# A two-layer cross-attention kernel: another order of the work of a group in its second layer

## Chip, cores and metric

One core of a Trainium2 chip runs the kernel. The metric is device time in microseconds (us) of one execution. TensorE (PE) multiplies matrices, VectorE (DVE), ScalarE (ACT) and GpSimd (POOL) work elementwise, and SyncE (SP) issues most DMAs.

## What is computed

Sixteen batch rows `x` of 256 positions and 320 channels pass through two cross-attention layers with 20 heads of 16 channels. The context has 256 tokens of 512 channels. Layer 1 (index 0) treats the first 77 tokens as text and the rest as image tokens; layer 2 (index 1) treats the last 4 as image tokens. The second layer, cut to what matters:

```python
q   = heads(hidden_states @ W_q)
k_t = heads(text_ehs @ W_k);  v_t = heads(text_ehs @ W_v)
probs_t  = softmax(einsum('bhsd,bhtd->bhst', q, k_t) * attn_scale)
text_out = einsum('bhst,bhtd->bhsd', probs_t, v_t)
k_ip = heads(ip_ehs @ W_k_ip);  v_ip = heads(ip_ehs @ W_v_ip)
attn_scores = einsum('bhsd,bhnd->bhsn', q, k_ip) * attn_scale
qsem = l2norm(einsum('bhst,bte->bhse', probs_t, text_ehs))
sem  = einsum('bhse,bne->bhsn', qsem, l2norm(ip_ehs))
probs_ip = softmax(attn_scores + 0.5 * sem) * spatial_mask
out = (text_out + einsum('bhsn,bhnd->bhsd', probs_ip, v_ip)) @ W_out + b_out + residual
```

The norm of `qsem` is found without forming it, from the probabilities and the products of tokens with each other (the Gram matrix of the context).

## The kernel before, in words

Each layer works in 80 *groups*: 16 batch rows by 5 groups of four heads. One *slot* of the main loop at the end of `xattn2` advances each of several groups by one stage; slots 0 to 79 are layer 1 (`slot0`), the next 80 and two more are layer 2 (`slot1`). The order of TensorE's instructions is the order in which the code emits them. The queues of the other four engines are ordered by the framework's scheduler, by the dependences and a planned time line, and then run strictly in that order.

In layer 2, a slot `k` holds, in the order of `slot1`:

- `attend1(k - 2)`: the values of the group two slots back. 16 matmuls onto 32-column tiles (L852) multiply the probabilities `P` by the tokens' values, and 8 more (L854, the *zone*) add the column sums of `W`, the norm's products. `settle1` then transposes and divides on VectorE (L898, L901, L902).
- `both1(k, 0)` and `both1(k, 1)`: the two halves of the 64-row work. Each has transposed scores of group `k` (L800, two PSUM banks, exponentials on ScalarE at L811 into `P`) and scores of group `k + 2` (L805), whose row maximum VectorE takes (L806). The scores have one PSUM buffer of two banks (`scores()`, `bufs=1`). Both kinds use 48 to 50 rows, two at a time in the upper and lower 64 rows of the array.
- `norm1(k - 1, u, n)`: the *block products*, the rounded probabilities (`R`) by blocks of the Gram matrix, four matmuls (n = 0) and three (n = 1) for each of two halves u (L839). VectorE multiplies each result by the remainder `W` (L842). The sum of both goes to GpSimd for u = 0 and to VectorE for u = 1 (L844); the zone matmuls read it.
- `rounded1(k, u)`: ScalarE rounds `P` (L829), GpSimd takes the remainder (L830).
- `stacks(k + 4)`: DMAs that load the queries and keys of a later group; `maxima(k + 2)`: two small matmuls (L817), a copy (L819) and two DMAs issued by ScalarE (L821) that put the maxima into the query stack.
- a number between the parts, such as `yield 0.33`, calls `fill`: all steps of the side tasks that are due by then are emitted. Each task has a list of due times: the next rows' keys (`keys1`), tokens' values and Gram matrix (`tokens1`), queries and image scores (`open1`, with the image keys of `image1`, L510), the image softmax (`image_softmax`), and the output projection (`close1`). Their matmuls are called *fillers* below.

Buffers decide what may overlap. The stacks of queries and keys, `qs` and `ks`, have four tiles each (`NR`), which layer 2 uses as eight half stacks in turn. `P` has four tiles, two for a group, so a group's exponentials overwrite the probabilities of the group two back, and `attend1(k - 2)` must come before `both1(k, 0)`:

```python
P[k, u] = buf("P", [128, 2, 2, S], bufs=SIZES["NP"])
```

Of the kernel before, what the change touches and what calls it, by code (L numbers as in the profile page):

```python
# [16 lines left out]
B = 16  # L17
# [31 lines left out]
def xattn2(  # L49
# [212 lines left out]
    wq, wo = [lambda s, k, m=slice(None): wqt[:, s, k, m]], []  # L262


    qs = [const_tile([128, 4, S], f"qs{i}", FR) for i in range(SIZES["NR"])]
    ks = [const_tile([128, 4, S], f"ks{i}", FR) for i in range(SIZES["NR"])]
    ind0 = buf("raw", [128, 512], bufs=SIZES["RAW"], name="ind0")[:2, :S]
    dma(ind0, ind0_d)
    ind0r = buf("mt", [8, S], FR, name="ind0r")[:2]
# [367 lines left out]

    def stacks1(k):
        b, g = divmod(k - NS, NG)
        n = 2 * SIZES["NR"]  # L640
        i = ((NS - SIZES["NR"]) % SIZES["NR"]) * 2 + (k - NS) % n
        Q, K = QK[k] = [x[i // 2 % SIZES["NR"]][:, 2 * (i % 2) : 2 * (i % 2) + 2] for x in (qs, ks)]
        get("k1", b)
        qd = get("o1", b)[0]
        for u in range(2):
            rows = slice(64 * u, 64 * u + XROW)
            hs = slice(4 * g + u, 4 * g + u + 3, 2)
            if k - NS < n:
                dma(K[64 * u + XROW : 64 * u + KS1], w1["ind"])
            dma(K[rows], stack_rows(kd[1][b][:, :, 0])[:, hs])  # L650
            dma(Q[rows], stack_rows(qd)[:, hs])
# [134 lines left out]
    def both1(k, t):  # L786

        a = k + 2 < 2 * NS and QK[k + 2] 
        c = NS <= k < 2 * NS and QK[k]
        if a:  # L790
            if t == 0:
                maxes[k + 2] = buf("mn", [128, 4, 4], FR, bufs=2)[:, :2]
            sp = scores()
        if c:
            st = [bank("T").rearrange("p (h t) -> p h t", h=2) for u in range(2)]
            lo = (0, DUP)[t]
            for j in range(2):
                for u in range(2):
                    rows = slice(64 * u, 64 * u + KS1)
                    mm(st[u][:, j], c[1][rows, j, lo : lo + 128], c[0][rows, j], start=True, stop=True)  # L800
        if a:
            for j in range(2):
                for u in range(2):
                    rows = slice(64 * u, 64 * u + XROW)
                    mm(sp[:, 2 * u + j], a[0][rows, j, t * 128 : (t + 1) * 128], a[1][rows, j], start=True, stop=True)  # L805
            anchor(nc.vector.tensor_reduce(maxes[k + 2][:, t], sp[:, :, :T1], axis=AX.X, op=ALU.max))  # L806
        if c:
            for u in range(2):
                if t == 0:
                    P[k, u] = buf("P", [128, 2, 2, S], bufs=SIZES["NP"])  # L810
                anchor(nc.scalar.activation(P[k, u][:, t], st[u], AF.Exp, scale=SCALE))  # L811

    def maxima1(k):
# [43 lines left out]
    def slot1(k):  # L857
        last = k - 1 if NS < k <= 2 * NS else None
        mine = k < 2 * NS
        if k == NS:  # L860
            yield lambda: maxima(k + 1)
        elif k == NS + 1:
            yield lambda: attend0(k - 2)
        else:
            yield lambda: attend1(k - 2)
        yield lambda: both1(k, 0)
        if last:
            yield lambda: norm1(last, 0, 0)
        yield 0.33
        if last:  # L870
            yield lambda: norm1(last, 0, 1)
        yield lambda: both1(k, 1)
        if mine:
            yield lambda: rounded1(k, 0)
        yield lambda: stacks(k + LEAD)
        if last:
            yield lambda: norm1(last, 1, 0)
        yield 0.67
        if last:
            yield lambda: norm1(last, 1, 1)  # L880
        if mine:
            yield lambda: rounded1(k, 1)
        yield lambda: maxima(k + 2)
        yield 1.0
# [89 lines left out]
    def open1(b):  # L974
# [2 lines left out]
        xs = split(x, tmask[:, 5:6], nc.gpsimd, "hq")  # L977
        yield
        get("w2")
        qh, qd = yield from queries(1, xs)  # L980

        kb = image1(b)
        yield
        sp = bank()[:, :S]
        prod(sp, lambda s, k: kb[:, s, k], lambda s, k: qh[:, s, k], 3)
# [48 lines left out]
    def shifted(n, *times):  # L1034

        return [RAMP(n + t) for t in times]
# [10 lines left out]
    for c in range(B // 2):  # L1047
# [8 lines left out]
        task(("v0", 2 * c + 1), shifted(n, -4, -3.8, -3.4), lambda b=2 * c + 1: values0_(b), *k)  # L1056
        for b, t in ((2 * c, (-7.4, -6.4, -6, -5.4, -5, -4.4, -3.4)), (2 * c + 1, (-2.4, -1.4, -1, -0.8, -0.4, 0, 1.2))):
            task(("s0", b), FIRST["s0"] if b == 1 else shifted(n, *t), lambda b=b: semantic0(b), ("q0", b), ("m0t", b))
            task(("c0", b), shifted(5 * b, *((5.6, 6, 6.6, 7.2, 7.6, 8.2) if b % 2 == 0 else (5.6, 6, 6.6, 7.2, 8.2, 9.2) if b < B - 1 else (6.33, 6.67, 7, 7.67, 8, 8.67))), lambda b=b: close0(b), ("w4", 0))
    for b in range(B):  # L1060
        n = NS + 5 * b
        task(("k1", b), shifted(n, -7, -6.67, -6.33, -5.67, -5, -4.67), lambda b=b: keys1(b), ("w2",), *([("t1", b - 1)] if b else []), *([("w4", 1)] if b > 2 else []))
        task(("t1", b), shifted(n, -3.67, -3, -2.67, -2.33), lambda b=b: tokens1(b), ("k1", b), ("w3", b % 2))
        task(("o1", b), shifted(n, -7.67, -7, -6.67, -5.33, -4.33, -4), lambda b=b: open1(b), ("w7",), ("c0", b), *([("o1", b - 1)] if b else []))
        task(("i1", b), shifted(n, 6.67, 6.67, 6.67, 6.67, 7.33, 7.33, 7.67, 7.67, 8, 8.33), lambda b=b: image_softmax(b, NG - 1 if b == B - 1 else 0), ("gathered", b), ("taken", B + b - 1), *([("i1a",)] if b == B - 1 else []))
        task(("c1", b), shifted(n + (1.67 if b > B - 3 else 0), 8.67, 9, 9.33, 10, 11.67, 13.33), lambda b=b: close1(b), ("i1", b), ("w4", 1))
    task(("i1a",), [2 * NS + 0.1], lambda: image_softmax(B - 1, 0, NG - 1), ("i1", B - 2))
    spread = lambda t, d, n: [t + d * i for i in range(n)]
    thirds = lambda n, t: [t + i // 3 + (0.2, 0.6, 1.0)[i % 3] for i in range(n)]
# [157 lines left out]
```

## Time and profile before

| what | value |
|---|---|
| median of three runs | 1540.75 us (1538.49 to 1541.03) |
| the profiled execution | 1543.74 us, its span 1542.0 us |
| layer 2 in that execution | first scores of layer 2 at 676 us, first transposed scores at 690 us |
| VectorE, ScalarE, GpSimd, share of the span | 78%, 62%, 75% |

The profile's groups are lists of instructions by source line, engine and tile, with the mean length of one. Starts in the timeline are measured; ends of matmuls are modelled. A row in brackets names what ended the idle time in front of it. Line numbers are those of the kernel before.

### The profile page before, as it was taken

The page shows a single profiled execution, that of the slowest core. Times are in us where ns is not written, and L with a number is a line of the kernel's source. Part 1 is how long each engine was busy: PE and PEld are TensorE (multiplying, and loading weights), DVE is VectorE, ACT ScalarE, POOL GpSimd, SP SyncE. Part 2 cuts the span into 40 slices and gives each one's busy share as a digit, 9 for nine tenths or more (in the row PEclk, how much of TensorE's full clock was granted, in tenths as well). Part 3 has the DMA queues.
Part 4 walks back from the last instruction along what each step waited for, and adds up shares of the span by engine and source line. Part 5 has one row for each costly group of instructions (what it writes and reads, how often), then busy time and mean ns, then how long its engine had stood idle before and what let it go on. Part 6 is the DMA issues. An engine that isn't in the chain of part 4 may idle for free.

```text
span 1542.0 us, 35152 instructions
## 1 busy us (share of the span) xinstructions
PE 1480.8 (96%) x12666; PEld 1200.5 (78%) x12666; DVE 1203.0 (78%) x2472; ACT 950.0 (62%) x2073; POOL 1155.2 (75%) x1161
## 2 busy tenths in 40 slices
PE   7889999999999998799999999999999999999997
PEld 6778888888888887677777777777777777777765
DVE  5567677767677779877888888888888888888796
ACT  5567676767677767655655555655555556556553
POOL 3359797979787868797777777777777777777685
PEclk9899999999999999999999999999999999999999
DMA  6756665656565665554443443334243434432301
GB/s 213 179 161 179 164 174 160 189 145 193 151 183 151 183 172 151 146 164 138 144 126 89 131 126 113 113 117 152 82 133 115 138 98 131 127 117 84 105 28 57
DMA packets 205626, 212.82 MB, mean 138 GB/s; under 512 B 28362, under 2 KB 189356, under 8 KB 205452
## 3 DMA queue, kind: packets, MB, share of 16 engines
q1 hardware_dynamic: 203712, 209.27, 46.9%
q8 instruction: 101, 1.65, 0.5%
q10 hardware_dynamic: 1740, 1.30, 0.3%
q14 instruction: 73, 0.60, 0.1%
HBM read 120.91 MB, written 88.18 MB: 136 GB/s over the span
## 4 chain that ended last, share of the span: by engine, by line
PE 86%; DVE 6%; ACT 3%; DMA 2%; issue 1%; POOL 1%; SPq 0%; ACTq 0%; POOLq 0%; DVEq 0%
PE X L212 23%; PE X L839 18%; PE X L532 11%; PE P L723 7%; PE S L662 5%; PE T L685 4%; PE T L800 4%; PE P L852 4%; PE P L854 3%; PE S L805 2%; PE X L960 1%; PE X L581 1%; DVE wt L844 1%; POOL P L691 1%; PE X L670 1%
## 5 line engine op out<-in xcount | busy, mean ns | idle before, releaser
L691 POOL TENSOR_TENSOR P<-P,rs 128x512 f32<-128x512 f32 x320 | 412.7, 1312 | 154.1 <-ACT P L688 114.8
L830 POOL TENSOR_TENSOR wt<-P,ctb 128x512 f32<-128x512 f32 x320 | 418.1, 1322 | 131.2 <-ACT ctb L829 131.0
L839 PE MATMUL X<-ctb,gm 128*128 128x512 f32 x1120 | 330.0, 412 | 0.0
L811 ACT ACTIVATE P<-T 128x512 f32<-128x512 f32 x320 | 174.1, 598 | 107.5 <-PE T L800 106.6
L688 ACT ACTIVATE P<-T 128x512 f32<-128x512 f32 x320 | 174.8, 593 | 101.2 <-PE T L685 91.2
L829 ACT ACTIVATE ctb<-P 128x512 fp32r<-128x512 f32 x320 | 195.4, 632 | 60.0 <-PE X L839 59.5
L839 PEld LDWEIGHTS X<-ctb,gm 128*128 128x128 f32 x1120 | 189.3, 188 | 45.3 <-issue 0.4
L806 DVE TENSOR_REDUCE mn<-S 128x4 fp32r<-128x1008 f32 x160 | 192.0, 1200 | 0.2 <-PE S L805 0.2
L842 DVE TENSOR_TENSOR wt<-X,wt 128x512 f32<-128x512 f32 x240 | 161.9, 679 | 12.1 <-PE X L839 11.1
L664 DVE TENSOR_REDUCE mn<-S 128x4 fp32r<-128x716 f32 x160 | 142.5, 890 | 0.0
L723 PE MATMUL P<-P,vr 128*32 128x256 f32 x1920 | 123.0, 387 | 7.8 <-DVE tmp L740 4.9
L662 PE MATMUL S<-ks,qs 125*128 125x256 f32 x640 | 115.6, 303 | 1.9 <-DVE mn L664 1.9
L532 PE MATMUL X<-hq,wE 128*128 128x256 f32 x768 | 110.4, 288 | 4.5 <-ACT hq L521 3.9
L662 PEld LDWEIGHTS S<-ks,qs 125*128 125x128 f32 x640 | 87.1, 191 | 34.8 <-issue 31.3
L532 PE MATMUL X<-ho,wF 128*128 128x256 f32 x768 | 108.9, 285 | 0.9 <-ACT mt L672 0.5
L532 PEld LDWEIGHTS X<-hq,wE 128*128 128x128 f32 x768 | 103.0, 194 | 8.2 <-ACT hq L521 4.3
L685 PE MATMUL T<-qs,ks 127*128 127x256 f32 x640 | 104.3, 286 | 1.9 <-DVE kst L148 1.9
L212 PE MATMUL X<-cta,wA 128*128 128x252 f32 (+1 forms) x720 | 100.2, 285 | 5.9 <-ACT wA L147 5.5
L532 PEld LDWEIGHTS X<-ho,wF 128*128 128x128 f32 x768 | 100.6, 190 | 5.2 <-DVE ho L762 0.7
L844 POOL TENSOR_TENSOR wt<-wt 128x512 f32<-128x512 f32 x80 | 103.8, 1298 | 0.4 <-DVE wt L842 0.4
L212 PEld LDWEIGHTS X<-cta,wA 128*128 128x128 f32 x720 | 93.1, 193 | 8.8 <-ACT wA L147 5.7
L800 PEld LDWEIGHTS T<-qs,ks 50*128 50x128 f32 x640 | 47.7, 184 | 61.7 <-issue 33.3
(202 smaller groups left out, 2996.5 us busy)
## 6 DMA issues: line engine op xcount, KB each, us to landing
qd<-q SPq DMA_DIRECT2D x96, 384.0 KB
kd<-kst SPq DMA_DIRECT2D x73, 256.0 KB
rawc<-in_cT_dram SPq DMA_DIRECT2D x60, 256.0 KB
qs<-qd SPq DMA_DIRECT2D x80, 192.0 KB
ks<-kd SPq DMA_DIRECT2D x80, 192.0 KB
ks<-kd SPq DMA_DIRECT2D x160, 96.0 KB
qs<-qd SPq DMA_DIRECT2D x160, 96.0 KB
kd<-kst SPq DMA_DIRECT2D x21, 512.0 KB
```

The lines of the kernel that those rows point to most:

```text
L212: last = mm(out, lhs(a, k), rhs(b, k), start=i == 0, stop=i == len(terms) - 1)
L532: mm(pp, w(s, k, slice(m * 128, (m + 1) * 128)), a[:, t], start=i == 0, stop=i == len(terms) - 1)
L662: mm(sp[:, h], Q[: XROW + T0, h, t * 128 : (t + 1) * 128], K[: XROW + T0, h], start=True, stop=True)
L685: mm(st[p][:, j], K[:KS0, 2 * p + j, t * 128 : (t + 1) * 128], Q[:KS0, 2 * p + j], start=True, stop=True)
L688: exp = anchor(nc.scalar.activation(pt, st[p], AF.Exp, scale=SCALE))
L691: anchor(nc.gpsimd.tensor_mul(pt, pt, rs[:, t : t + 1].to_broadcast([128, 2, S])))
L723: mm(pv[32 * s : 32 * s + 32, o : o + S], v[:, vt, h : h + 32], P[k, s // 2][:, t, s % 2], start=vt < 2, stop=vt != 1,)
L806: anchor(nc.vector.tensor_reduce(maxes[k + 2][:, t], sp[:, :, :T1], axis=AX.X, op=ALU.max))
L811: anchor(nc.scalar.activation(P[k, u][:, t], st[u], AF.Exp, scale=SCALE))
L829: nc.scalar.activation(R[k, u][:, t], P[k, u][:, t], AF.Copy, scale=0.5)
L830: anchor(nc.gpsimd.tensor_sub(W[k, u][:, t], P[k, u][:, t], f(R[k, u][:, t])))
L839: mm(yp, gm[:, gb], R[k, u][:, kt], start=i == 0, stop=i == len(blocks[n]) - 1)
```

## The change

In `slot1`, the first half of the 64-row work now comes first, then the values, then the second half, and the two sets of block products follow one another. The last values of layer 1 move from slot 81 to slot 80. Every third group's `P` lives in the fourth tile of `qs` and `ks`, which layer 2 then no longer uses as a stack: six half stacks remain, and `P` is three groups deep. `open1` makes the image keys ahead of the queries' projection. The steps of the second output projection after the first are due a third of a slot later, and the last projection of layer 1 is due two thirds of a slot earlier.

```diff
--- before.py
+++ after.py
@@ -262,8 +262,9 @@
     wq, wo = [lambda s, k, m=slice(None): wqt[:, s, k, m]], []
 
 
-    qs = [const_tile([128, 4, S], f"qs{i}", FR) for i in range(SIZES["NR"])]
-    ks = [const_tile([128, 4, S], f"ks{i}", FR) for i in range(SIZES["NR"])]
+    last_stack = lambda shape, dtype, u: sb.tile(shape, dtype, tag=("qsl", "ksl")[u], name=("qsl", "ksl")[u], bufs=1)
+    qs = [const_tile([128, 4, S], f"qs{i}", FR) for i in range(SIZES["NR"] - 1)] + [last_stack([128, 4, S], FR, 0)]
+    ks = [const_tile([128, 4, S], f"ks{i}", FR) for i in range(SIZES["NR"] - 1)] + [last_stack([128, 4, S], FR, 1)]
     ind0 = buf("raw", [128, 512], bufs=SIZES["RAW"], name="ind0")[:2, :S]
     dma(ind0, ind0_d)
     ind0r = buf("mt", [8, S], FR, name="ind0r")[:2]
@@ -637,9 +638,9 @@
 
     def stacks1(k):
         b, g = divmod(k - NS, NG)
-        n = 2 * SIZES["NR"]
-        i = ((NS - SIZES["NR"]) % SIZES["NR"]) * 2 + (k - NS) % n
-        Q, K = QK[k] = [x[i // 2 % SIZES["NR"]][:, 2 * (i % 2) : 2 * (i % 2) + 2] for x in (qs, ks)]
+        n = 2 * (SIZES["NR"] - 1)
+        i = (k - NS) % n
+        Q, K = QK[k] = [x[i // 2][:, 2 * (i % 2) : 2 * (i % 2) + 2] for x in (qs, ks)]
         get("k1", b)
         qd = get("o1", b)[0]
         for u in range(2):
@@ -807,7 +808,7 @@
         if c:
             for u in range(2):
                 if t == 0:
-                    P[k, u] = buf("P", [128, 2, 2, S], bufs=SIZES["NP"])
+                    P[k, u] = buf("P", [128, 2, 2, S], bufs=SIZES["NP"]) if (k - NS) % 3 else last_stack([128, 2, 2, S], F32, u)
                 anchor(nc.scalar.activation(P[k, u][:, t], st[u], AF.Exp, scale=SCALE))
 
     def maxima1(k):
@@ -859,17 +860,17 @@
         mine = k < 2 * NS
         if k == NS:
             yield lambda: maxima(k + 1)
-        elif k == NS + 1:
-            yield lambda: attend0(k - 2)
-        else:
+        yield lambda: both1(k, 0)
+        if k == NS:
+            yield lambda: attend0(k - 1)
+        if k > NS + 1:
             yield lambda: attend1(k - 2)
-        yield lambda: both1(k, 0)
+        yield lambda: both1(k, 1)
         if last:
             yield lambda: norm1(last, 0, 0)
         yield 0.33
         if last:
             yield lambda: norm1(last, 0, 1)
-        yield lambda: both1(k, 1)
         if mine:
             yield lambda: rounded1(k, 0)
         yield lambda: stacks(k + LEAD)
@@ -977,9 +978,8 @@
         xs = split(x, tmask[:, 5:6], nc.gpsimd, "hq")
         yield
         get("w2")
+        kb = image1(b)
         qh, qd = yield from queries(1, xs)
-
-        kb = image1(b)
         yield
         sp = bank()[:, :S]
         prod(sp, lambda s, k: kb[:, s, k], lambda s, k: qh[:, s, k], 3)
@@ -1056,14 +1056,14 @@
         task(("v0", 2 * c + 1), shifted(n, -4, -3.8, -3.4), lambda b=2 * c + 1: values0_(b), *k)
         for b, t in ((2 * c, (-7.4, -6.4, -6, -5.4, -5, -4.4, -3.4)), (2 * c + 1, (-2.4, -1.4, -1, -0.8, -0.4, 0, 1.2))):
             task(("s0", b), FIRST["s0"] if b == 1 else shifted(n, *t), lambda b=b: semantic0(b), ("q0", b), ("m0t", b))
-            task(("c0", b), shifted(5 * b, *((5.6, 6, 6.6, 7.2, 7.6, 8.2) if b % 2 == 0 else (5.6, 6, 6.6, 7.2, 8.2, 9.2) if b < B - 1 else (6.33, 6.67, 7, 7.67, 8, 8.67))), lambda b=b: close0(b), ("w4", 0))
+            task(("c0", b), shifted(5 * b, *((5.6, 6, 6.6, 7.2, 7.6, 8.2) if b % 2 == 0 else (5.6, 6, 6.6, 7.2, 8.2, 9.2) if b < B - 1 else (5.67, 6, 6.33, 7, 7.67, 8))), lambda b=b: close0(b), ("w4", 0))
     for b in range(B):
         n = NS + 5 * b
         task(("k1", b), shifted(n, -7, -6.67, -6.33, -5.67, -5, -4.67), lambda b=b: keys1(b), ("w2",), *([("t1", b - 1)] if b else []), *([("w4", 1)] if b > 2 else []))
         task(("t1", b), shifted(n, -3.67, -3, -2.67, -2.33), lambda b=b: tokens1(b), ("k1", b), ("w3", b % 2))
         task(("o1", b), shifted(n, -7.67, -7, -6.67, -5.33, -4.33, -4), lambda b=b: open1(b), ("w7",), ("c0", b), *([("o1", b - 1)] if b else []))
         task(("i1", b), shifted(n, 6.67, 6.67, 6.67, 6.67, 7.33, 7.33, 7.67, 7.67, 8, 8.33), lambda b=b: image_softmax(b, NG - 1 if b == B - 1 else 0), ("gathered", b), ("taken", B + b - 1), *([("i1a",)] if b == B - 1 else []))
-        task(("c1", b), shifted(n + (1.67 if b > B - 3 else 0), 8.67, 9, 9.33, 10, 11.67, 13.33), lambda b=b: close1(b), ("i1", b), ("w4", 1))
+        task(("c1", b), shifted(n + (1.67 if b > B - 3 else 0), 8.67, 9.33, 9.67, 10.33, 11.67, 13.33), lambda b=b: close1(b), ("i1", b), ("w4", 1))
     task(("i1a",), [2 * NS + 0.1], lambda: image_softmax(B - 1, 0, NG - 1), ("i1", B - 2))
     spread = lambda t, d, n: [t + d * i for i in range(n)]
     thirds = lambda n, t: [t + i // 3 + (0.2, 0.6, 1.0)[i % 3] for i in range(n)]
```

## The prediction

> **What bounds the kernel now.** I read the page first (the 40 slices, the chain that ended last), then a stretch of layer 2 as a window, then the timeline of TensorE, VectorE and ScalarE over five slots in the middle of layer 2.
>
> ```profile
> span 1542.0 us, 35152 instructions
> PE 86%; DVE 6%; ACT 3%; DMA 2%; issue 1%; POOL 1%; SPq 0%; ACTq 0%; POOLq 0%; DVEq 0%
> ```
> TensorE (PE) sets the end: 86% of the chain lies on it. So the question is only what the change does to TensorE's own time: gaps, and what each change of shape costs.
>
> ```profile
> 1034.04:1087.10 53.06, 52.53 (x435) 40.59 (x428) 44.88 (x84) 30.49 (x69) 39.99 (x44) 1.00 0.39 120
> ```
> The columns are stretch, length, then busy time of PE, PEld, DVE, ACT, POOL, and the granted clock, 1.00. Layer 2 has 80 slots (a slot handles one group of four heads), and five slots, one batch row, repeat every 53.06 us. VectorE (DVE) is at 44.88 of 53.06, 85%: the second most loaded, and a queue in order.
>
> Here is TensorE over one slot boundary, from the last three block matmuls of a group (L839 x3) on:
>
> ```profile
> 1032.76 0.86 PE L839 MATMUL X<-ctb,gm 128*128 128x512 f32 x3
> 1033.46 0.28 PE L817 MATMUL X<-ident_r,mn 128*4 128x128 f32 x2
> 1033.67 1.07 PE L852 MATMUL P<-P,v1t 128*32 128x256 f32 x16
> 1034.56 0.59 PE L854 MATMUL P<-wt,zone 128*32 128x256 f32 x2
> 1035.68 0.63 PE L854 MATMUL P<-wt,zone 128*32 128x256 f32 x6 [0.53 <-DVE wt L844]
> 1036.24 0.50 PE L800 MATMUL T<-qs,ks 50*128 50x256 f32 x4
> 1036.58 0.40 PE L805 MATMUL S<-ks,qs 48*128 48x256 f32 x4
> 1036.91 1.20 PE L839 MATMUL X<-ctb,gm 128*128 128x512 f32 x4
> 1037.95 1.12 PE L532 MATMUL X<-ho,wF 128*128 128x256 f32 x8
> ```
> and, later in the same slot,
>
> ```profile
> 1039.86 0.86 PE L839 MATMUL X<-ctb,gm 128*128 128x512 f32 x3
> 1040.65 0.50 PE L800 MATMUL T<-qs,ks 50*128 50x256 f32 x4
> ```
> The time from one start to the next is the true cost of a row; the printed length is modelled. Two losses show. First, a wait: the zone matmuls (L854) take 1.68 us to the next row (34.56 to 36.24) where their two rounds of four need 0.55, because the last sum of the group before (L844 on VectorE) comes late. Second, changes of shape, below.
>
> **The waits that go.** At a second boundary of each five the same wait is short: 0.91 less 0.55, 0.36 us. The other three have none, and the last slots, which have little work to put between, wait at each.
>
> ```profile
> 1045.06 0.98 PE L854 MATMUL P<-wt,zone 128*32 128x256 f32 x8
> 1045.97 0.50 PE L800 MATMUL T<-qs,ks 50*128 50x256 f32 x4
> ...
> 1485.49 0.59 PE L854 MATMUL P<-wt,zone 128*32 128x256 f32 x2
> ...
> 1486.95 0.50 PE L800 MATMUL T<-qs,ks 50*128 50x256 f32 x4
> ```
> 1486.95 less 1485.49 less 0.55 is 0.91 us. Taken so over all 80 slots the excess is 30 us: 1.5 in each of 14 batch rows (21), about 2 in the first slots, about 7 in the last seven. In the new order the first half's 64-row work (L800, L805) stands between the maxima and the values, so this wait has 0.67 us more cover, and the values a third score buffer (the freed stack), without which they could not wait.
>
> **Changes of shape.** Call F the full array, C the 32-column tiles (L852, L854), R the 64-row tiles (L800, L805). Three block matmuls take 0.70 before a full-array row (32.76 to 33.46) but 0.79 before R (39.86 to 40.65): F to R costs 0.09. The two maxima matmuls cost 0.21 before C (33.46 to 33.67), and 0.11 before a full-array row:
>
> ```profile
> 1064.18 0.86 PE L839 MATMUL X<-ctb,gm 128*128 128x512 f32 x3
> 1064.88 0.28 PE L817 MATMUL X<-ident_r,mn 128*4 128x128 f32 x2
> 1064.99 1.28 PE L212 MATMUL X<-q,kb 128*128 128x256 f32 x9
> 1066.20 1.07 PE L852 MATMUL P<-P,v1t 128*32 128x256 f32 x16
> ```
> so F to C is 0.10. Four block matmuls after R take 1.04 (36.91 to 37.95) where four at 0.70/3 take 0.93: another 0.11 for the first weights after R to F. Before, a slot goes F-C-R-F-R-F; after, F-R-C-R-F, with both R parts around C and the two sets of block matmuls next to each other. Gone are one F to C (0.10) and one R to F (about 0.09, taken equal to F to R, plus 0.11); new is R to C, which no row shows: between nothing and 0.20, and I take 0.10, as F to C. That saves 0.2 us a slot (0.10 to 0.30), some 15 us in 78 slots (8 to 23). [...]
>
> **The new wait.** Both halves of a group's scores are written to PSUM in front of one reduction each:
>
> ```profile
> L806 DVE TENSOR_REDUCE mn<-S 128x4 fp32r<-128x1008 f32 x160 | 192.0, 1200 | 0.2 <-PE S L805 0.2
> ```
> 1.20 us each, against 0.33 for the matmuls. There is one score buffer, and in the program as built the second half's score matmuls wait for the first half's reduction. Before, about 4 us of block products and fillers lay between the halves. After, only values, zone and the transposed scores do. [...]
>
> When does TensorE want the second scores? Count from the start of the last block matmuls, n. 0.70 + 0.11, the filler F, 0.10 for F to R, then transposed scores 0.34, scores 0.33, values 0.89, zone 0.55, transposed scores 0.34: n + 3.36 + F. The reduction stands in VectorE's new order right behind the last sum (L844), or behind what the scheduler put there. The zone's wait releases 0.05 after a VectorE row ends, and the next row starts 0.60 after the sum does. By boundary, with the rows of before:
>
> ```profile
> 1034.95 0.68 DVE L844 TENSOR_TENSOR wt<-wt,X 128x512 f32<-128x512 f32 x1
> ```
>
> ```profile
> 1042.60 1.04 PE L839 MATMUL X<-ctb,gm 128*128 128x512 f32 x3
> 1044.70 0.65 DVE L844 TENSOR_TENSOR wt<-wt,X 128x512 f32<-128x512 f32 x1
> ```
> (1) Behind the token products: F is 0, the sum starts at n + 2.19, the reduction runs 2.79 to 3.99, TensorE goes on at 4.04 instead of 3.36: 0.68 us. (2) F is 0, the sum at 2.10: 3.95 instead of 3.36, 0.59 us. Both contain what is left of the zone's wait.
>
> ```profile
> 1052.92 0.86 PE L839 MATMUL X<-ctb,gm 128*128 128x512 f32 x3
> 1054.74 1.55 PE L212 MATMUL X<-cta,wA 128*128 128x252 f32 x12
> 1056.22 1.07 PE L852 MATMUL P<-P,v1t 128*32 128x256 f32 x16
> ...
> 1054.85 1.30 ACTq L821 DMA_DIRECT2D qs<-mt  x2
> 1056.33 0.37 ACT L147 CAST kst<-X 128x252 fp32r<-128x252 f32 x1 [1.51 <-PE X L212]
> 1056.73 0.42 DVE L148 TENSOR_TENSOR kst<-X,kst 128x252 fp32r<-128x252 f32 x1 [0.74 <-ACT kst L147]
> ```
> (3) The filler is the keys, 1.48 less 0.10, 1.38; wanted at 4.74. In VectorE's new order the key's low half (L148) stands before the reduction; it needs ScalarE's cast (L147), which stands behind two DMA issues that end at n + 3.23. The new order has one more cast ahead of them, 0.2. So cast 3.5, L148 3.9, reduction 4.25 to 5.45: 0.76, at least 0.56 without that cast; I take 0.7.
>
> ```profile
> 1065.87 0.69 DVE L844 TENSOR_TENSOR wt<-wt,X 128x512 f32<-128x512 f32 x1
> 1066.47 1.15 DVE L510 TENSOR_TENSOR kb<-kip,kmask 128x384 fp32r<-128x384 f32 x1
> 1067.54 0.44 DVE L987 STREAM_TRANSPOSE si<-X 128x256 f32<-128x256 f32 x1
> 1067.91 1.27 DVE L510 TENSOR_TENSOR kb<-kip,kmask 128x384 fp32r<-128x384 f32 x1
> 1069.10 0.44 DVE L898 STREAM_TRANSPOSE nt<-P 128x256 f32<-128x256 f32 x1
> ```
> (4) n is 1064.18, F 1.21 less 0.10, 1.11; wanted at 4.47. The two image key products of a later batch row and a transpose stand between sum and reduction, in the new order as in the old: the earlier emission does not move them, since they wait for the buffer that the projection here sets free. So the reduction starts where L898 did, n + 4.92, ends at 6.12, and TensorE waits until 6.17: 1.70 us. Before, TensorE needed nothing from VectorE for some 3 us more, which hid them. This occurs in 12 batch rows; the last ones have no later keys.
>
> (5) The filler, twelve value matmuls, is longer than that of (3), so the sum (done by n + 2.4, as at (4)) is earlier than the first scores, and the reduction waits for these alone. TensorE comes back 2.11 after their start (0.33, 0.89, 0.55, 0.34); reduction and hand-over, 1.2 and about half a us, are over by then: no wait.
>
> **The sum.** A batch row with keys: 0.68 + 0.59 + 0.7 + 1.70 = 3.67 new, 1.5 and 5 x 0.2 gone: +1.17, times 12, +14. Two without keys: 1.97 less 2.5, -0.5 each, -1. The first and last twelve slots: 9 us of waits become about 2 (with nothing between, the sum starts near n + 1.6 as at (4), the reduction ends at 3.4, and is awaited for 0.1), and 2.4 of shape go: about -9. Together about +4. The remaining edits I cost at nothing: the second projection's steps, emitted a third of a slot later, are the same matmuls in another gap, covered by TensorE's queue; the ring of stacks shrinks from eight half stacks to six, but a load still reuses a stack two slots after its last reader; if a load did come late, every score matmul behind it on TensorE would. Layer 1 keeps its order but for its last values and projection, a slot or less earlier. On its own time, 1543.74 us with 1542.0 of span, that makes 1548; on the median of 1540.75, which lies 3 lower, 1545.
>
> **Rivals.** (A) Faster: VectorE comes earlier. Its reduction no longer stands between the block products of one group, so the last sum may start at n + 1.7 at (1) and (2), as at (4), not 2.1 to 2.2. That takes 0.5 from each of two boundaries, 14 us in all: 1531, or 1523 with R to C free as well. For it: at (2) a reduction stands just before. Against: at (1) two products for the tokens still stand before the sum. It decides if the sum comes at n + 1.7. (B) Slower by more: VectorE falls behind. Each slot now has transposes, reciprocal and a second reduction (about 2.1 us) ahead of the first block product, so block outputs hold their PSUM banks longer. At (1) this product would end near n + 6.8, and TensorE comes back for the bank at about n + 8; over 1.2 us of further lag it waits. At 0.2 us a slot, 16 us: 1562. Against: VectorE keeps some 15% free. (C) It does nothing: the zone's waits return as score waits of the same length and shapes cost what they did: 1541.
>
> **How the numbers follow.** The forecast 0.46 (1545, own range 1539 to 1553), A 0.29, B 0.2, C 0.05. About 0.2%, 3 us, is what can be told from no change. Of the forecast a third lies within that: same 0.15 + 0.05 = 0.2; slower 0.31 + 0.2 = 0.51; faster 0.29. The range reaches to A's and B's middles: 1529 to 1562; it holds both bounds of R to C (+8, -8).
>
> **What would show it.** Right: zone matmuls with hardly a wait; score matmuls that wait for the reduction, 20 us over the boundaries with key products, longest 1.7; block matmuls in rows of seven or with 0.93 for the second set; the five slots at 54.2 us where keys are made and 52.5 where not. Wrong: score waits under 1 us at the key products, or waits on transposed scores, block outputs or loads above 5 us in all.

## The result, and the profile after

| | before | after |
|---|---|---|
| median of 7 runs (lowest to highest), us | 1542.71 (1538.49 to 1546.82) | 1553.21 (1546.31 to 1559.68) |
| ratio to before, 95% interval | | 1.0070 (1.0042 to 1.0097) |
| the profiled execution: its time, its span, us | 1543.74, 1542.0 | 1549.21, 1547.4 |

The change makes the kernel slower, by 0.7%: 10.5 us between the medians. The profiled executions lie only 5.5 us apart; that difference is accounted for below. The page of the changed kernel, its span and the shares of the chain that ended last, by engine:

```profile
span 1547.4 us, 35237 instructions
PE 70%; DVE 12%; POOL 6%; ACT 5%; DMA 4%; issue 2%; ACTq 1%; SPq 0%; POOLq 0%; DVEq 0%
```
TensorE's share of the chain falls from 86% to 70%, VectorE's doubles to 12%, and GpSimd's grows to 6%: TensorE now stops for them. Five slots as a window (stretch, length, busy time of PE, PEld, DVE, ACT, POOL, granted clock, DMA share, GB/s):

```profile
1031.11:1084.99 53.88, 51.95 (x429) 41.15 (x428) 44.27 (x84) 30.29 (x68) 40.25 (x44) 1.00 0.38 118
```
53.88 us against 53.06. TensorE's rows got shorter (51.95 against 52.53), so it is gaps that make the stretch longer. The waits of the matmuls, from the view of waits of the changed kernel (engine, tile and line that waits, what released it, us in total, times, longest):

```profile
PEld S L806 <- DVE mn L807: 28.6, 43, 1.4
PE S L806 <- DVE mn L807: 18.9, 26, 1.2
PEld P L855 <- POOL wt L845: 18.0, 20, 1.5
PEld P L855 <- DVE wt L845: 6.7, 16, 1.1
```
The first two rows are the new wait: score matmuls (L806) for the reduction (L807). Weight loads and matmuls are listed apart and overlap (41.15 and 51.95 us busy in the 53.88 above), so the rows aren't added. From start to start of the matmuls, the score wait is about 27 us in all, and before it was none. The zone matmuls (L855) still wait, but more for GpSimd's sum (L845, first half) than for VectorE's. Most line numbers are one higher than before. What the prediction and some expectations call a third score buffer is the third buffer of the probabilities `P`; the scores keep their single one.

The four boundaries with a wait, from TensorE's timeline of the changed kernel (start, length, engine, line, operation, tiles; in brackets the idle time before the row):

```profile
1039.05 1.09 PE L855 MATMUL P<-wt,zone 128*32 128x256 f32 x8
1040.07 0.51 PE L801 MATMUL T<-qs,ks 50*128 50x256 f32 x4
1040.63 0.50 PE L806 MATMUL S<-ks,qs 48*128 48x256 f32 x4
1041.06 1.20 PE L840 MATMUL X<-ctb,gm 128*128 128x512 f32 x4
...
1047.67 1.07 PE L853 MATMUL P<-P,v1t 128*32 128x256 f32 x16
1049.13 0.64 PE L855 MATMUL P<-wt,zone 128*32 128x256 f32 x8 [0.39 <-POOL wt L845]
...
1060.65 0.51 PE L801 MATMUL T<-qs,ks 50*128 50x256 f32 x4
1061.47 0.50 PE L806 MATMUL S<-ks,qs 48*128 48x256 f32 x4 [0.31 <-DVE mn L807]
...
1071.99 0.50 PE L801 MATMUL T<-qs,ks 50*128 50x256 f32 x4
1073.67 0.50 PE L806 MATMUL S<-ks,qs 48*128 48x256 f32 x4 [1.17 <-DVE mn L807]
```
Start to start, less what the row needs (zone 0.55, transposed scores 0.34, values 0.89): boundary (1) loses 0.47 at the zone and 0.22 at the scores, (2) 0.57 at the zone and nothing at the scores, (3) 0.48 and (4) 1.34 at the scores. A score row behind a wait also takes 0.43 instead of 0.33 (1040.63 to 1041.06); its weight load waits for the reduction as well, 0.26 us in this place. At (2) it is GpSimd's sum that ends last, as its timeline shows:

```profile
1047.80 1.28 POOL L845 TENSOR_TENSOR wt<-wt 128x512 f32<-128x512 f32 x1
```
It ends at 1049.08, and the zone goes on at 1049.13. Boundary (4) in VectorE's timeline:

```profile
1069.57 0.69 DVE L845 TENSOR_TENSOR wt<-wt,X 128x512 f32<-128x512 f32 x1
1070.18 0.61 DVE L511 TENSOR_TENSOR kb<-kip,kmask 128x384 fp32r<-128x384 f32 x1
1070.71 0.44 DVE L987 STREAM_TRANSPOSE si<-X 128x256 f32<-128x256 f32 x1
1071.08 1.42 DVE L511 TENSOR_TENSOR kb<-kip,kmask 128x384 fp32r<-128x384 f32 x1
1072.42 1.19 DVE L807 TENSOR_REDUCE mn<-S 128x4 fp32r<-128x1008 f32 x1
```
The two image key products and a transpose stand between the sum and the reduction, 2.24 us, while the score matmuls wait. A wait of over 1 us at the scores occurs in exactly 12 places, one in each batch row with later keys.

One more place stands outside the rows, where layer 1 gives way to layer 2. TensorE and VectorE there, in the changed kernel:

```profile
691.81 0.40 PE L806 MATMUL S<-ks,qs 48*128 48x256 f32 x4
695.54 0.51 PE L801 MATMUL T<-qs,ks 50*128 50x256 f32 x4 [3.33 <-DVE ho L763]
696.65 0.79 PE L806 MATMUL S<-ks,qs 48*128 48x256 f32 x4 [0.61 <-DVE mn L807]
697.38 2.07 PE L840 MATMUL X<-ctb,gm 128*128 128x512 f32 x4
699.25 3.40 PE L212 MATMUL X<-wC,cta 128*128 128x320 f32 x12
```

```profile
692.81 1.07 DVE L954 TENSOR_TENSOR rs<-rs,nt 128x384 f32<-128x384 f32 x1 [1.46 <-DMA nt<-in_bmask_dram]
693.80 0.54 DVE L511 TENSOR_TENSOR kb<-kip,kmask 128x384 fp32r<-128x384 f32 x1
...
695.41 1.19 DVE L807 TENSOR_REDUCE mn<-S 128x4 fp32r<-128x1008 f32 x1
```
A VectorE product (L954, the image values of the first batch row by their mask) waits for the mask's DMA, the key products follow it, and then come a product of an output projection (L763) and the reduction. TensorE stands still for 3.33 us, until L763 is done, then 0.61 for the reduction behind it, and afterwards its rows take up to twice as long: four block matmuls 2.07 us, not 1.20, twelve value matmuls (L212) 3.40, not 1.9. The granted clock from 690 to 700 us is 0.82, where before it was 1.00.

### The profile page after: what moved, and what is told of

It reads as the page before. It is cut to its first block, busy times and chain, and to the rows that moved or that the text cites. A ratio compares the mean times of both kernels' runs of the same rounds, so it can differ in the third digit from the quotient of the medians.

```text
span 1547.4 us, 35237 instructions
## 1 busy us (share of the span) xinstructions
PE 1470.2 (95%) x12666; PEld 1210.1 (78%) x12666; DVE 1193.7 (77%) x2472; ACT 947.5 (61%) x2073; POOL 1156.9 (75%) x1161
## 4 chain that ended last, share of the span: by engine, by line
PE 70%; DVE 12%; POOL 6%; ACT 5%; DMA 4%; issue 2%; ACTq 1%; SPq 0%; POOLq 0%; DVEq 0%
PE X L212 21%; PE X L840 13%; PE X L533 10%; PE P L724 6%; PE S L663 5%; PE T L686 4%; POOL wt L831 3%; DVE mn L807 3%; PE S L806 2%; DVE kb L511 2%; ACT ctb L830 2%; PE T L801 2%; POOL wt L845 2%; PE P L855 1%; PE P L853 1%
## 5 line engine op out<-in xcount | busy, mean ns | idle before, releaser
L831 POOL TENSOR_TENSOR wt<-P,ctb 128x512 f32<-128x512 f32 x212 | 273.6, 1310 | 110.0 <-ACT ctb L830 109.9
L840 PE MATMUL X<-ctb,gm 128*128 128x512 f32 x1120 | 309.9, 406 | 0.0
L689 ACT ACTIVATE P<-T 128x512 f32<-128x512 f32 x320 | 174.6, 593 | 96.9 <-PE T L686 90.6
L840 PEld LDWEIGHTS X<-ctb,gm 128*128 128x128 f32 x1120 | 196.9, 189 | 40.9 <-issue 0.4
L807 DVE TENSOR_REDUCE mn<-S 128x4 fp32r<-128x1008 f32 x160 | 191.4, 1196 | 17.5 <-PE S L806 17.4
L830 ACT ACTIVATE ctb<-P 128x512 fp32r<-128x512 f32 x212 | 123.6, 625 | 58.1 <-PE X L840 56.2
L812 ACT ACTIVATE P<-T 128x512 f32<-128x512 f32 x212 | 114.3, 592 | 44.6 <-PE T L801 44.2
L212 PE MATMUL X<-cta,wA 128*128 128x252 f32 (+1 forms) x720 | 100.8, 286 | 6.3 <-ACT wA L147 6.0
L831 POOL TENSOR_TENSOR wt<-qsl,ctb 128x512 f32<-128x512 f32 x54 | 69.2, 1294 | 49.0 <-ACT ctb L830 49.0
L845 POOL TENSOR_TENSOR wt<-wt 128x512 f32<-128x512 f32 x80 | 103.6, 1294 | 0.0
L212 PEld LDWEIGHTS X<-cta,wA 128*128 128x128 f32 x720 | 92.0, 193 | 8.1 <-ACT wA L147 6.2
L735 DVE STREAM_TRANSPOSE nt<-P 128x512 f32<-128x512 f32 x80 | 57.0, 712 | 43.9 <-PE P L724 43.8
L664 DVE TENSOR_REDUCE mn<-S 128x4 fp32r<-128x308 f32 x160 | 74.2, 464 | 20.3 <-PE S L663 20.2
L724 PEld LDWEIGHTS P<-P,vr 128*32 128x32 f32 x1920 | 55.6, 110 | 42.1 <-POOL P L692 4.1
```

The costliest lines, as they stand in the source:

```text
L212: last = mm(out, lhs(a, k), rhs(b, k), start=i == 0, stop=i == len(terms) - 1)
L689: exp = anchor(nc.scalar.activation(pt, st[p], AF.Exp, scale=SCALE))
L724: mm(pv[32 * s : 32 * s + 32, o : o + S], v[:, vt, h : h + 32], P[k, s // 2][:, t, s % 2], start=vt < 2, stop=vt != 1,)
L830: nc.scalar.activation(R[k, u][:, t], P[k, u][:, t], AF.Copy, scale=0.5)
L831: anchor(nc.gpsimd.tensor_sub(W[k, u][:, t], P[k, u][:, t], f(R[k, u][:, t])))
L840: mm(yp, gm[:, gb], R[k, u][:, kt], start=i == 0, stop=i == len(blocks[n]) - 1)
```

## Where the profiled executions differ

Taken from the start of the values (L852, L853) of one slot to that of another, in us:

| stretch | before | after | difference |
|---|---|---|---|
| to the first values of layer 2 | 707.0 | 708.7 | +1.7 |
| the first ten slots | 105.15 | 104.23 | -0.9 |
| 50 slots, ten batch rows with keys | 530.35 | 539.99 | +9.6 |
| ten slots, two batch rows without | 106.09 | 104.89 | -1.2 |
| the rest, to the last values | 89.39 | 85.50 | -3.9 |

The first row hides something. Near the end of layer 1, in the kernel before, one VectorE product took 4.98 us beside three pairs of GpSimd's products, and TensorE waited for it. Before, then the same product after:

```profile
623.28 4.98 DVE L148 TENSOR_TENSOR wE<-rawc,wE 128x384 fp32r<-128x384 f32 x1
...
620.41 7.44 POOL L691 TENSOR_TENSOR P<-P,rs 128x512 f32<-128x512 f32 x6
...
630.00 2.79 PE L723 MATMUL P<-P,vr 128*32 128x256 f32 x24 [4.88 <-DVE tmp L740]
```

```profile
623.51 1.30 DVE L148 TENSOR_TENSOR wE<-rawc,wE 128x384 fp32r<-128x384 f32 x1
```
It ended at 628.26, 0.41 us after GpSimd's run of products (627.85). The same instruction takes 4.97 to 5.11 us in the profiles of five of the kernels here, with the old slot order and the new, and 1.42 us or less in the others: it falls one way or the other, and the 24 value matmuls behind it run at half speed as well (2.79 us, otherwise 1.50). By the profiles that is some 4 to 5 us, which the profiled execution of the changed kernel was spared: the kernel with the moved steps alone (below) runs the same instructions as the kernel before until 778 us; it had the short product, 1.30 us, and its first values come 4.2 us earlier. With it, the difference would be about 10 us, as between the medians. That the runs without a profile differ by this product too is likely, and was not shown.

## The experiments

Ratios are to the kernel before, with 95% intervals; "row" is five slots in the middle of layer 2, from values to values: 53.04 before, 53.9 after. Boundary numbers are the prediction's.

**The key products.** The changed kernel, with its two key products held behind the VectorE work written before them.

```diff
 def image1(b):
-    nc.vector.tensor_mul(kb[:, s], ...)
+    queued(nc.vector.tensor_mul(kb[:, s], ...))
```

> The changed kernel, with the two image key products held to the place where they are written, so that they land behind a second reduction of another slot and not between the last sum and the first reduction at boundary (4). My theory (the single score buffer, step (4)): the score matmuls that in the changed kernel's trace wait 1.34 us there wait 0.1 or less, in 12 batch rows; 12 x 1.3 is 16 us, so some 1537 against the changed kernel's 1553. Rival (VectorE has too much to do as such, wherever the two products stand): the wait turns up at another boundary and the time stays at 1550 to 1555. Second rival (the products are late for the image scores where they stand now): a new wait of the image score matmuls on them, and more than 1553.

Measured 1547.12 us, 1.0018 (0.9998 to 1.0037): 0.5% less than the changed kernel, where 1% was expected. The wait itself went entirely, as TensorE's timeline of this kernel shows at (4):

```profile
1077.08 0.51 PE L801 MATMUL T<-qs,ks 50*128 50x256 f32 x4
1077.42 0.40 PE L806 MATMUL S<-ks,qs 48*128 48x256 f32 x4
1077.75 1.21 PE L840 MATMUL X<-ctb,gm 128*128 128x512 f32 x4
```
0.34 and 0.33: no wait, and none of over 1 us at any score matmul of the kernel. A row takes 52.6 us, 1.3 less than the changed kernel's, so the mechanism is shown and my theory right in layer 2. But layer 2's first values come at 718.7 us, not 708.7: the L148 product above took 5.1 us, and another VectorE row (L435) 2.3 instead of 0.2. Do the products held during layer 1 cost that? The next kernel holds them only for batch rows that are made in layer 2.

```diff
-    queued(nc.vector.tensor_mul(kb[:, s], ...))
+    (queued if b > 1 else lambda i: i)(nc.vector.tensor_mul(kb[:, s], ...))
```

> The changed kernel with the image key products held to their written place for the batch rows from the third on, that is in layer 2 alone; those of the first two rows, which are made while layer 1 ends, stay as in the changed kernel. In the run with all of them held, the rows of layer 2 took 52.6 us as predicted, but layer 1 ended some 5 us later. My theory (the shifted order at the change of layers costs that, through VectorE instructions that run 2 to 4 us too long beside GpSimd): 1540 to 1544, 3 to 7 us under that run. Rival (the end of layer 1 differs from run to run and has nothing to do with the held products): 1546 to 1549 again.

Measured 1539.11 us, 0.9981 (0.9964 to 0.9999): rows of 52.6 again, first values at 706.0. So holding the products of layer 1 did cost some 6 us by the ratios, and in layer 2 the score wait at (4) alone, 12 times 1.3 us, is worth more than the whole loss of the change: without it, the change is a gain of 0.2%, whose interval just leaves out none at all.

**The mask product.** It stands ahead of the sum in each batch row and waits for a DMA, in the rows 0.36 us at most in the changed kernel's profile. Held like the keys, alone and with them:

```diff
-    nc.vector.tensor_mul(vb, vb, w1["bmask"])
+    queued(nc.vector.tensor_mul(vb, vb, w1["bmask"]))
```

> The changed kernel, with the product that masks the image values (L954) held to its written place, so that it stands behind a second reduction and no longer between the last products of a group and its sum, where it waits for a DMA. Theory (a term that my prediction lacks: this product stalls VectorE while the DMA is late, the sum and the reduction behind it, and so the score matmuls; it was 0.36 us once in the profiled run and is longer in others): the median falls by 4 to 6 us, to 1547 to 1549, and the runs lie closer together than the changed kernel's 13 us from lowest to highest. Rival (the profiled run is short by chance, the DMA has no part): 1551 to 1555 with the same spread.

> The changed kernel with both of these: the two image key products and the product that masks the image values held to their written places. If the score wait at boundary (4) and the DMA's lateness are separate terms, the savings add up: 16 and 5 less than 1553, about 1532, faster than the kernel before (1543) by 0.7%. If the one hides the other (the VectorE queue recovers at the same place), no better than the better of the two alone. If VectorE's load as such decides: 1550 to 1555.

1551.02 us, 1.0046 (1.0028 to 1.0064), and 1545.59 us, 1.0014 (0.9995 to 1.0033). The first gained 2 us by the medians and 4 by the ratios, with intervals that overlap, less than expected, its twelve runs still 8.9 us apart; its rows take 53.8, 0.1 less. So the DMA's lateness is no large term of the rows. With both held, rows take 53.0, 0.4 more than with the keys alone: two savings, each with another place in the queue, didn't add up.

**The old slot order.** The changed kernel with a slot's order as before, to see what the rest costs.

```diff
-        yield lambda: both1(k, 0)
-        if k == NS:
-            yield lambda: attend0(k - 1)
-        if k > NS + 1:
+        elif k == NS + 1:
+            yield lambda: attend0(k - 2)
+        else:
             yield lambda: attend1(k - 2)
-        yield lambda: both1(k, 1)
+        yield lambda: both1(k, 0)
...
+        yield lambda: both1(k, 1)
```

> The changed kernel, with the order of a slot as it was before (second half's 64-row work behind the values), and all else of the change kept: the freed stack as a third score buffer, six half stacks, the earlier image keys, the later projection steps. My theory (the order of the slot makes the score waits, the rest is nothing by itself): about the kernel before, 1541 to 1545, with no score matmul that waits for a reduction. Rival (the shorter ring of stacks, or the moved projection steps, cost by themselves): 1548 or more, with waits on loads or on the rounded values.

Measured 1570.67 us, 1.0169 (1.0143 to 1.0194): my theory fell, 27 us on the wrong side. One half of it held: no score matmul waits for a reduction here, so the slot's order makes those waits. But the rest of the change is not nothing, it costs more than the order. Set beside the kernel before, which has the same order of matmuls, its rows (54.4) lose at (2) and (3), where image value and projection products had stood behind the maxima. So the suspect was the moved projection steps, which I had costed at nothing. That part alone, in the kernel before:

```diff
-shifted(..., 8.67, 9, 9.33, 10, 11.67, 13.33), lambda b=b: close1(b)
+shifted(..., 8.67, 9.33, 9.67, 10.33, 11.67, 13.33), lambda b=b: close1(b)
```

> The kernel before, with one part of the change alone: the second projection's steps of the rows (close1) emitted at the changed kernel's times, so that image values and eight projection products leave the place behind the maxima of boundaries (2) and (3). The run with the old slot order was 27 us slower than before, and row for row its extra stands at these two boundaries (zone matmuls 0.48 us later at (2) and 0.61 at (3), 0.27 beside them: 1.34 in a row of five slots). My theory now (the moved steps are no free edit: they were the cover of the sum): 12 to 14 rows of 1.3 us, 1558 to 1562. Rival (the shorter ring of stacks or the freed stack as a score buffer cost it): 1541 to 1545.

Measured 1559.86 us, 1.0115 (1.0091 to 1.014), with rows of 54.4. TensorE at (2) in this kernel:

```profile
1047.15 0.59 PE L854 MATMUL P<-wt,zone 128*32 128x256 f32 x2
1047.98 0.63 PE L854 MATMUL P<-wt,zone 128*32 128x256 f32 x6 [0.23 <-DVE wt L844]
1048.55 0.50 PE L800 MATMUL T<-qs,ks 50*128 50x256 f32 x4
```
The zone matmuls take 1.40 us, where they took 0.91 with the image values ahead of them. So the steps cost 17 us in the old order, shown alone. The kernel with the old slot order loses about 10 more, hardly any of it in the rows: its first values come at 708.5 us, not 702.8, since the mask product waits 3.43 us for its DMA where the layers change, and TensorE 3.75 for the reduction behind it. The other 4 or so stay open. So the loss at the change of layers does not need the new slot order: another part of the change is enough for it, and which one was not tested.

**The steps back, in the new order.** The same line undone in the changed kernel, then in the one with the keys held in layer 2.

> The changed kernel, with the second projection's steps emitted at the times of before, and all else changed. If the moved steps cost in the new order what they cost in the old one, 1.3 us in each row: 1536. My theory: at boundary (3) eight more projection products stand ahead of the second scores, so its wait (0.48 and 0.10 for the first weights) goes, but at (2) the program as built puts a transpose's sum and the image values' copy (0.85 us) ahead of the reduction there, and its wait grows by about 0.5; together within 3 us of the changed kernel, 1550 to 1556. The mask product stands ahead of the block products again, so the DMA is no longer waited for: 1 to 3 us less.

> The run before this one, with the projection's steps at the times of before as well. If the steps' times are worth nothing in the new order: the same as that run. If they take the wait from boundary (3) and give 0.5 back at (2): the same within 3 us. If they are worth 1.3 us in a row: 16 us less, 1526.

1555.24 us, 1.0089 (1.0063 to 1.0114), and 1536.43 us, 0.9954 (0.9935 to 0.9973). In the new order the steps' place is worth little, as expected: the first kernel is within 3 us of the changed one, the second 3 to 4 us below the one with the keys held, and the intervals overlap both times. But the wait at (2) wasn't the one I named. TensorE in the second kernel:

```profile
1043.43 0.28 PE L818 MATMUL X<-ident_r,mn 128*4 128x128 f32 x2
1044.95 0.70 PE L961 MATMUL X<-rs,rs 128*128 128x256 f32 x2 [1.23 <-DMA out_dram<-xc]
1045.58 0.50 PE L801 MATMUL T<-qs,ks 50*128 50x256 f32 x4
```
The image values (L961) themselves wait 1.3 us there, and the zone behind them no longer. The profile names a DMA that writes an output in this row, which they don't read; their weight loads wait for ScalarE in 12 places, by the view of waits:

```profile
PEld X L961 <- ACT mt L820: 17.1, 12, 1.4
```
L820 is the copy of the maxima, which reads what the row before (L818) wrote to PSUM. Here it ends at 1044.90, 0.05 us before the image values start, so it is probably the bank of the maxima that they wait for, and not one that VectorE empties. At (3) the wait is gone. So the next kernel leaves only the projection products of (3) at the times of before:

```diff
-8.67, 9, 9.33, 10, 11.67, 13.33
+8.67, *((9.33, 9.67) if b < B - 2 else (9, 9.33)), 10, 11.67, 13.33
```

> The run with the image keys held in layer 2 and the steps back, with two of these steps a third of a slot later again: the image values stand where the changed kernel has them, and only the eight projection products stay behind the maxima of boundary (3); the last two rows keep the times of before. In the run that had all steps back, the four image value matmuls behind the maxima of (2) waited 1.30 us for a bank that VectorE empties late, in every row. My theory: that wait goes, boundary (3) keeps its 0.6 us gain, and a row takes 52.0 to 52.1 us against 52.75: 12 x 0.7 = 8 less, 1528. If the image values' wait is only passed on to the next boundary (2), where the zone and the transposed scores then wait as they do with the steps late: 0.97 less 0.55 and 0.2 come back, and the row is 52.4: 1533.

Measured 1529.13 us, 0.9914 (0.9893 to 0.9934), by the ratios 6 us less than the kernel before it, for 8 expected. The image values no longer wait, and the row has the length that was expected; as a window it is nearly all busy TensorE:

```profile
1031.93:1083.97 52.04, 51.94 (x433) 41.26 (x431) 44.13 (x84) 30.50 (x68) 39.52 (x44) 1.00 0.40 122
```

**The change of layers.** One VectorE instruction moved, in that kernel and in the changed one.

```diff
-    nc.vector.tensor_mul(vb, vb, w1["bmask"])
+    (queued if b == 0 else lambda i: i)(nc.vector.tensor_mul(vb, vb, w1["bmask"]))
```

> The run before this one, with a single VectorE instruction of the program moved: the product that masks the image values of the first batch row (L954) stands some 100 instructions later. Before, it stood in the first slots of layer 2 ahead of a reduction and waited 1.3 to 1.5 us there for the mask's DMA; TensorE had a gap of 2.4 to 3.7 us and then ran some 6 us with rows twice as long. My theory (a one-off of the new order at the change of layers, made larger by TensorE's slow rows behind the gap): gap under 1.6 us and no slow rows, 4 to 7 us less than that run. If the slow rows come with any gap there: 1 to 2 us less. Rival (another instruction is waited for at that place): no difference.

> The changed kernel with only that one instruction moved. My theory: the gap of 3.6 us at the first reductions of layer 2 shrinks to 1.4 to 2.2 (the key products of the second row still stand ahead of the reduction there), the slow rows behind it become fewer, and the median falls by 2 to 6 us, to 1547 to 1551. Rival (all that the change lost is in the rows of layer 2): 1552 to 1554.

1525.21 us, 0.9887 (0.9863 to 0.9911), the fastest here, and 1550.06 us, 1.0054 (1.0035 to 1.0073). TensorE where the layers change, in the first:

```profile
691.08 0.51 PE L801 MATMUL T<-qs,ks 50*128 50x256 f32 x4 [0.18 <-DVE ho L763]
692.20 0.50 PE L806 MATMUL S<-ks,qs 48*128 48x256 f32 x4 [0.62 <-DVE mn L807]
692.64 1.20 PE L840 MATMUL X<-ctb,gm 128*128 128x512 f32 x4
693.67 1.92 PE L212 MATMUL X<-wC,cta 128*128 128x320 f32 x12
```
The gap, 1.96 us in the kernel above it and 3.33 in the changed one, is 0.18, and the rows behind it run at full speed: the one instruction was what TensorE waited for, through VectorE's queue. The median is 4 us lower, the low end of what was expected. How much of that comes from here is not shown: the profiled execution of the kernel above had the long L148 product, this one had not, and this one has slow rows in its first ten slots instead (108.4 us against 103.4), behind idle times that both have. The first of them, in this kernel and then in the one above:

```profile
723.51 1.08 PE L855 MATMUL P<-wt,zone 128*32 128x256 f32 x8 [1.25 <-POOL wt L845]
725.67 2.07 PE L840 MATMUL X<-ctb,gm 128*128 128x512 f32 x4
...
733.01 0.64 PE L855 MATMUL P<-wt,zone 128*32 128x256 f32 x8 [1.24 <-POOL wt L845]
734.25 1.21 PE L840 MATMUL X<-ctb,gm 128*128 128x512 f32 x4
```
In the changed kernel the key products still stand ahead of the reduction there, and the gap is 2.05, with slow rows still behind it. The gain of 2.5 us by the ratios is not clear of noise: the intervals overlap, and the profiled executions differ by 0.5 us at the first values (708.2 against 708.7).

**The price of the single buffer.** Both halves' 64-row work directly behind each other, after the values.

```diff
-        yield lambda: both1(k, 0)
         if k == NS:
             yield lambda: attend0(k - 1)
         if k > NS + 1:
             yield lambda: attend1(k - 2)
+        yield lambda: both1(k, 0)
         yield lambda: both1(k, 1)
```

> The changed kernel with the values ahead of both halves' 64-row work, so that the second half's follows the first's directly: transposed scores of 0.34 us are then all that lies between the two score groups. It shows the price of the single score buffer by itself. Theory: in every slot the second scores wait for the whole first reduction, 1.2 us and about 0.1 of hand-over less 0.34, so 0.95 to 1.1 us in 80 slots (some 80 us, where the changed kernel's waits are some 50 in all with those of the first weights), the zone waits of before come back (some 20 us), and a change of shape in each slot goes (8 to 16): 1585 to 1615. Rival (scores don't wait for the reduction): no more than 1553.

A single run, 1741.69 us: the sign as expected, the size at least three times too small (32 to 62 us more than the changed kernel were expected, 188 came). TensorE in a slot of it, and in another:

```profile
1134.27 0.51 PE L806 MATMUL S<-ks,qs 48*128 48x256 f32 x4 [1.35 <-DVE mn L807]
1134.70 1.83 PE L840 MATMUL X<-ctb,gm 128*128 128x512 f32 x4
...
1163.02 0.80 PE L806 MATMUL S<-ks,qs 48*128 48x256 f32 x4 [2.34 <-DVE mn L807]
1163.74 2.07 PE L840 MATMUL X<-ctb,gm 128*128 128x512 f32 x4
```
The wait is 1.4 us in the one and 2.3 in the other, not 1.0, and behind both of these gaps TensorE's rows are again up to twice as long. Of the 192 us by which the profiled execution is longer than the changed kernel's, about half is idle time of TensorE (from 690 us on, 146 us against 41); the rest goes with slow rows, at a granted clock of 0.91 in that stretch against 0.99.

## Why the prediction was right, and where it wasn't

The forecast was 1545 us and slower as the likeliest sign; measured were 1553 us, inside the range of 1529 to 1562, and at the upper end of the forecast's own, 1539 to 1553. The forecast change of +4 us is +10.5 between the medians. So the mechanism and the sign were right, and that the number lies in the range owes something to luck: the range reaches to the middles of the rivals, and a term of some 6 us was left out.

- **The new wait** was right. It is the single score buffer: the second scores wait for the first reduction, in all 12 batch rows with keys, and the kernel with the keys held shows that it goes when the reduction comes earlier.
- **Its four terms**, 3.67 in a row: (1) 0.69 for the 0.68 of the sum, two thirds of it still at the zone; (3) 0.48 for 0.7; (4) 1.34 for 1.70, since the reduction started at n + 4.55 and not at 4.92. (2) has the size (0.57 for 0.59) by luck, with the wrong cause: it is the zone that waits, for GpSimd's sum of the first half, which the prediction left out. With 0.1 more for the score row behind three of them, 3.4.
- **Changes of shape** were right: the block matmuls of a slot took 1.04, 1.63 for seven and 0.70 in the changed kernel (1074.10 to 1075.13, 1076.90 to 1078.53, 1079.49 to 1080.18), 3.37 in all, where four sets took 3.56. That is 0.2 in a slot, and a score row takes 0.33 before the values, as it did before block matmuls (R to C adds nothing to be seen).
- **The row**: +1.17 was forecast with keys and -0.5 without. Measured is +0.96 over ten rows (typically 53.88 less 53.04, +0.84, and up to 54.54 in three), and -0.6.
- **The step that failed** is the third line of the sum, "The first and last twelve slots ... about -9", with the sentence behind it that costs the remaining edits at nothing. The end did save 3.9 us. But where the layers change, VectorE's queue in the changed kernel has a late DMA and two key products ahead of what TensorE waits for, and TensorE's slow rows behind the gap made it more: the kernel before with the moved steps alone, which has the old order and was spared the long L148 product too, has its first values at 702.8 us against 708.7, 5.9 later, 0.67 of them because the values now stand later in a slot. That term was missing. The new slot order is not what it takes, since the run with the old slot order and the rest of the change has a gap of 3.75 us there too; which of the other edits makes it stays open.
- **One sign of being right did not come**: "zone matmuls with hardly a wait". From start to start they still lose 22 us in layer 2, of 30 before. And the waits over 1 us at the key products add up to 16 us with a longest of 1.35, for 20 and 1.7.
- **The moved projection steps at nothing** was wrong as a statement, though it cost the sum little: alone they cost 17 us, since they were the cover of the sum at (2) and (3). In the new order undoing them all gains next to nothing; undoing the half at (3) gains.
- **Image keys emitted earlier** don't change the order on VectorE at boundary (4), as the prediction says; they were not tried by themselves. **The shorter ring of stacks** was not tried by itself; no wait on a load appears at the score matmuls.
- **Rivals.** A needed the sum at n + 1.7 at (1) and (2). It started at n + 2.19 and n + 2.12, so A fell. B needed waits for the banks of block outputs, 16 us of them; all that block matmuls lose in layer 2 is 4.6 us, for whatever reason, so its mechanism is not there. C fell with the rows. What the prediction called a wrong sign, score waits under 1 us at the key products, didn't come: they are 1.33 to 1.35.

## What to carry to other kernels

When the two writers of a single buffer are moved closer, count all that stands ahead of its reader on the reader's engine: here 2.2 us of work for a later row decided between 0.2% faster and 0.7% slower, and holding it in another place cost one line. Before calling a moved filler free, look at which wait it covers: the same three numbers cost 17 us in one order and nothing in the other. And take the stretch where two phases meet by itself, since waits that happen once there may be longer than any in the steady rows, here 3.33 us against 1.35.

## What was not expected of the hardware

Some gaps cost TensorE more than their length here. Behind idle times of 1.96 to 3.75 us at the change of layers, rows took up to twice as long for some 4 to 7 us: in the changed kernel, behind 3.33 us, twelve value matmuls 3.40 us instead of 1.9, at a granted clock of 0.82 from 690 to 700 us. In the kernel with both halves adjacent the same followed 1.35 and 2.34 us, and two gaps of 0.55 and 0.56 us close together, behind which four block matmuls took 2.07 us instead of 1.20. The 1.17 to 1.19 us at boundary (4) left the rows behind it as they were in all 12 places (four block matmuls 1.19 to 1.20 us). The length does not decide alone: 1.25 us in the first ten slots of the fastest kernel was followed by slow rows, and 1.24 at the same place in the kernel it was made from was not. The mean granted clock was 0.94 in the profiled execution of the kernel with adjacent halves, and 0.98 to 0.99 in the others. What decides whether rows turn slow, no run here shows.

One VectorE product took far longer beside GpSimd in one execution than in another: L148 took 4.98 us in the kernel before, until 0.41 us after GpSimd's run of six products was over, and 1.30 in the kernel with the moved steps alone, whose instructions are the same up to there. In the changed kernel it took 1.30 as well, beside a run of six that took 8.11 us instead of 7.44. The long one started 2.87 us into the run and lasted across several of its products; what held it up, no trace here shows.
